# Two KAN halves in four column groups, clears on VectorE, and bank copies booked a turn ahead: one change to a macaron block on one Trainium2 core

## The chip, the cores and the metric

The kernel runs on one core of one Trainium2 chip. A core has TensorE (PE, with its weight loads listed as PEld), VectorE (DVE), ScalarE (ACT), GpSimd (POOL) and the DMA queues, the most used of which is that of SyncE (SP). The metric is the device time of one execution in microseconds; less is better. Before the change it is 1758.36 us, the median of three runs (1757.0 to 1758.48).

## The reference

The input x is 16 batch rows of 512 tokens of width 128, float32. Six residual steps follow one another:

```python
x = x + 0.5 * KAN(layernorm(x))            # first KAN
x = x + attention(layernorm(x))            # 16 heads of 8, 4 kv heads, causal, rope
x = x + 0.5 * KAN(layernorm(x))            # second KAN, the same weights
x = x + 0.5 * MoE(layernorm(x))            # 8 experts, 128 tokens each
x = x + recurrence(layernorm(x))           # a gated linear scan over tokens
x = x + 0.5 * MoE(layernorm(x))
```

The KAN is the part that the change rewrites. With M = 64 and 16 inner units for each m:

```python
s = x @ Win + bin_                          # (.., 64)
h = relu(s[..., None] * W1 + b1)            # (.., 64, 16)
g = einsum('btmh,mh->btm', h, W2) + b2      # (.., 64)
out = g @ Wout + bout
```

## The kernel before, in words

**Layout of a KAN.** One batch row is handled at a time. `norm` gives the normalised row, `turned` transposes it on PE (line 288) and ACT copies it out as `kan_xT` (line 292). One matmul (line 303) against `win`, which holds Win twice side by side, gives s for 64 values of m on 2 x 64 partitions. ACT copies it to `kan_s` (307). Eight relus on ACT (329) each make one 128 x 512 tile `kan_h`: partitions 0 to 63 hold inner unit t, partitions 64 to 127 inner unit t + 8. After every second relu, two matmuls of 64 columns (335) sum a pair of tiles into the two halves of the bank `ps_kg`; `w2d` holds diagonal weights. So a KAN has one matmul at 303 and eight at 335, that is four pairs. ACT copies `ps_kg` out as gT (340), four matmuls with `wout` follow (346), and DVE adds the result to x (349). A float32 matmul appears as two PE records in the profile.

**Attention.** `attn_in` projects q, k and v (384 to 404), applies rope on DVE, adds on POOL (399, 423), and `parts` splits q and k into three bfloat16 parts: an ACT cast (356), a POOL subtraction (359), an ACT cast (362), a POOL subtraction (365). They go to HBM and back into the operand tiles `QP` and `KP` through the SP queue. `maxima` computes scores (PE 550) and row maxima (DVE 555, 560); `weights` computes transposed scores (608), exponentials (ACT 611) and the causal mask (POOL 613); `outputs` multiplies by v with four 32-column groups side by side (631).

**Order of the work.** The order of PE, ACT, DVE and POOL is fixed by generators that emit instructions as they are stepped. One `turn` steps one bank of `weights` of batch row b and one bank of `maxima` of row b + 1, and then every side generator once: KANs, norms, projections. A row has 44 turns. I call the 44 turns with the exponentials of row b "step b". In a turn, `need` lets a side generator wait until its work fits into what is left in `room`, whose budget `MOST` per turn is 1.5 us on PE, 1.15 on DVE, 0.85 on ACT, 1.45 on POOL; `take` subtracts without waiting, at the moment when the copy is emitted. `bank` waits until one of two general PSUM banks is free and PE has room. Pacing holds in steps 0 to 15 only. One KAN at a time owns `ps_kg` (`kan_held`), and its relu t is not emitted before 15 t / 8 turns after its first.

**Stages.** Start: constants, first KANs of rows 0 to 2, `attn_in` of rows 0 and 1, with `finish(first, second)` at its end. Fill: the maxima of row 0. Steps 0 to 15. Tail: `experts`, with the recurrences beside them. `prepare` makes the constants that the first KAN waits for (`rbias`, `kcst`, `w2d`, the centred projections) and clears the padding rows of the ten `QP` tiles on POOL (493) and of the three `KP` tiles on DVE (495, 496).

Of the kernel before, what the change touches and what calls it, by code (L numbers as in the profile page):

```python
# [16 lines left out]
P = 128  # L17
# [4 lines left out]
HALF = 8  # L22
# [22 lines left out]
def tile_macaron(  # L45
# [51 lines left out]
    with ExitStack() as ph:  # L97
# [5 lines left out]
        hp = ph.enter_context(tc.tile_pool(name="p1_h", bufs=4))  # L103
# [14 lines left out]
        win = cst.tile([D, 2, M], F32, name="win")  # L118
        binc = cst.tile([P, 1], F32, name="binc")
        kw1 = cst.tile([P, HALF], F32, name="kw1")  # L120
        kb1 = cst.tile([P, HALF], F32, name="kb1")
        kw2 = cst.tile([P, HALF], F32, name="kw2")
        nc.scalar.dma_start(out=win, in_=win_in.unsqueeze(1).to_broadcast([D, 2, M]))
        nc.scalar.dma_start(out=kw1, in_=kw1_in.rearrange("m (a h) -> a m h", a=2))
        nc.scalar.dma_start(out=binc, in_=bin_in.unsqueeze(0).to_broadcast([2, M]))
        nc.scalar.dma_start(out=kb1, in_=kb1_in.rearrange("m (a h) -> a m h", a=2))
        nc.scalar.dma_start(out=kw2, in_=kw2_in.rearrange("m (a h) -> a m h", a=2))
        kb2 = cst.tile([M, 1], F32, name="kb2")
        nc.scalar.dma_start(out=kb2, in_=kb2_in.unsqueeze(1))
        wout = cst.tile([P, D], F32, name="wout")  # L130
        nc.scalar.dma_start(out=wout, in_=wout_in.unsqueeze(0).to_broadcast([2, M, D]))
# [3 lines left out]
        rbias = cst.tile([P, HALF], F32, name="rbias")  # L135

        w2d = cst.tile([P, HALF, M], F32, name="w2d")
        eye2 = cst.tile([P, M], F32, name="eye2")
# [16 lines left out]
        nc.sync.dma_start(out=rope, in_=rope_in)  # L155
        for b in range(1, B):
            load(b)
# [52 lines left out]

        def refill():
            now[0] += 1
            room.update(MOST)
# [8 lines left out]
        def bank(shape, dtype, name, work=0.0):  # L222


            while held[0] == 2 or (paced[0] and work > room["pe"]):
                yield
            room["pe"] -= work
            held[0] += 1
            return mm.tile(shape, dtype, name=name, tag="mm")
# [55 lines left out]
        def turned(src, name, pool):  # L285
            ps = yield from bank([P, NT, P], F32, "ps_t", 0.55)
            for c in range(NT):
                nc.tensor.transpose(ps[:, c, :], src[:, c, :], ident)
            yield
            dst = pool.tile([P, S], F32, name=name)  # L290
            take(act=0.6)
            nc.scalar.copy(dst, ps.rearrange("p c q -> p (c q)"))
            freed()
            yield
            yield from rest(1)
            yield
            return dst

        def kan(b):

            _, xT = yield from norm(x[b])
            ps = yield from bank([P, S], F32, "ps_s", 0.9)
            nc.tensor.matmul(ps, lhsT=win.rearrange("d a m -> d (a m)"), rhs=xT, start=True, stop=True)
            yield
            sk = w2p.tile([P, S], F32, name="kan_s")
            take(act=0.6)
            nc.scalar.copy(sk, ps)
            freed()
            yield
            while kan_held[0]:  # L310
                yield
            kan_held[0] = 1
# [4 lines left out]
            for t in range(HALF + 1):  # L317
                while now[0] < begin + 15 * t // 8:
                    yield
                pair = t % 2 == 0 and t > 0  # L320
                work = {"act": 0.8} if t < HALF else {}
                if pair:
# [4 lines left out]
                if t < HALF:  # L327
                    h = hp.tile([P, S], F32, name="kan_h")
                    nc.scalar.activation(h, sk, AF.Relu, bias=rbias[:, t : t + 1], scale=kw1[:, t : t + 1])  # L329
                    hs.append(h)  # L330
                if t == 1:
                    nc.gpsimd.tensor_tensor(x[b], x[b], kcst.unsqueeze(1).to_broadcast([P, NT, D]), ALU.add)
                if pair:
                    for i in range(2):
                        nc.tensor.matmul(pg[i * M : (i + 1) * M, :], lhsT=w2d[:, t - 2 + i, :], rhs=hs[t - 2 + i],  # L335
                                         start=(t == 2), stop=(t == HALF))
                yield
            gT = hp.tile([P, S], F32, name="kan_h")
            take(act=0.6)
# [4 lines left out]
            po = yield from bank([P, NT, D], F32, "ps_ko", 0.9)  # L344
# [3 lines left out]
            take(dve=0.7)  # L348
# [4 lines left out]
        def parts(r, dst, copies, **work):  # L353
# [4 lines left out]
            yield from need(pool=1.15)  # L358
            nc.gpsimd.tensor_tensor(r, r, dst[:, 0, :], ALU.subtract)
            yield  # L360
            yield from need(**work)
            copies(dst[:, 1, :], r)
# [12 lines left out]
        def attn_in(b, st):  # L375
# [7 lines left out]
            pa = yield from bank([P, S], F32, "ps_pa", 0.9)  # L383
            nc.tensor.matmul(pa, lhsT=wq.rearrange("k h d -> k (h d)"), rhs=xT, start=True, stop=True)
            yield
            take(dve=0.7)
            nc.vector.tensor_mul(ta, pa, rope[:, 0, :])
            freed()
            pb = yield from bank([P, S], F32, "ps_pb", 0.9)
            nc.tensor.matmul(pb, lhsT=wqr.rearrange("k h d -> k (h d)"), rhs=xT, start=True, stop=True)  # L390
            yield
            take(dve=0.7)
            nc.vector.tensor_mul(tb, pb, rope[:, 1, :])
            freed()
            pk = yield from bank([2 * KR, S], F32, "ps_pk", 0.9)
# [4 lines left out]
            take(dve=0.7)  # L400
            nc.vector.tensor_mul(ka, pk[0:KR, :], rope[0:KR, 0, :])
            pv = yield from bank([P, NT, KR], F32, "ps_v", 0.9)
# [3 lines left out]
            take(dve=0.7)  # L406
            nc.vector.tensor_mul(kb, pk[KR : 2 * KR, :], rope[KR : 2 * KR, 1, :])
            freed()
            qp_steps = parts(ta, qpart, nc.scalar.copy, act=0.6)
            step(qp_steps)  # L410
# [10 lines left out]
            def keys():  # L421
                yield from need(pool=1.25)
                nc.gpsimd.tensor_tensor(ka, ka, kb, ALU.add)
                yield
                yield from parts(ka, kpart, nc.scalar.copy, act=0.6)

            yield from together(qp_steps, keys())
# [24 lines left out]
        def center_win():  # L452
            psc = yield from bank([P, 2 * M], F32, "ps_kc0")
            centered(psc, win.rearrange("d a m -> d (a m)"))
            freed()

        def prepare():

            nc.vector.scalar_tensor_tensor(rbias, in0=kw1, scalar=binc, in1=kb1, op0=ALU.mult, op1=ALU.add)
            nc.gpsimd.memset(ones, 1.0)  # L460
            nc.gpsimd.memset(onec, 1.0)
            psc = yield from bank([1, D], F32, "ps_kc")
            nc.tensor.matmul(psc, lhsT=kb2, rhs=wout[0:M, :], start=True, stop=True)
            nc.vector.tensor_add(kcr, psc, bout)
            freed()
            yield
# [5 lines left out]
            nc.vector.tensor_add(eye2, ident[:, 0:M], ident[:, M:P])  # L472
            for u in range(HALF):
                nc.vector.tensor_scalar(w2d[:, u, :], eye2, kw2[:, u : u + 1], 0.5, ALU.mult, ALU.mult)
                if u == HALF // 2:
                    yield
# [11 lines left out]
            make_identity(nc, identb)  # L488
            nc.gpsimd.memset(causal[:, 0 : S - P], 0.0)
            make_causal_mask(nc, own, NEG)  # L490
            yield
            for i in range(NQP):
                nc.gpsimd.memset(QP[i][MXR - 32 : MXR, :, :], 0.0)
                if i < NKP:
                    nc.vector.memset(KP[i][MXR - 32 : MXR, :, :], 0.0)
                    nc.vector.memset(KP[i][MXR : MXR + 3, :, :], 1.0)
                yield
# [4 lines left out]
            yield  # L502
# [61 lines left out]
        def max_rows(b, half, maxs):  # L564
# [14 lines left out]
            pm = yield from bank([3 * H2, NT, P], BF16, "ps_m", 0.3)  # L579
# [3 lines left out]
            mr = w2p.tile([3 * H2, S], BF16, name="mr")  # L583
            take(dve=0.4)
# [34 lines left out]
        def outputs(b, st, r):  # L619
# [20 lines left out]
            pq = yield from bank([P, NT, NG, 32], F32, "ps_oq", 0.5)  # L640
# [4 lines left out]
            take(dve=0.55)  # L645
# [6 lines left out]
        def stage_out(b, st):  # L652
# [3 lines left out]
            po = yield from bank([P, NT, D], F32, "ps_o", 0.9)  # L656
# [3 lines left out]
            take(dve=0.7)  # L660
# [11 lines left out]
        def gated(k, b):  # L672
# [3 lines left out]
            ps = yield from bank([P, NT, E], F32, "ps_g", 0.9)  # L676
# [3 lines left out]
            take(dve=0.2)  # L680
# [468 lines left out]
```

## Time and profile before

The profiled execution took 1763.15 us, 1761.4 of it as span between first and last instruction, at a mean granted TensorE clock of 0.968.

| Stage (us of the span) | length | PE busy | DVE busy | ACT busy | POOL busy | PE clock |
|---|---|---|---|---|---|---|
| Start, 0 to 76.1 | 76.1 | 41.2 | 35.9 | 28.8 | 42.0 | 0.91 |
| Fill, 76.1 to 127.6 | 51.5 | 39.1 | 38.3 | 16.7 | 17.5 | 0.72 |
| Steps 0 to 2, 127.6 to 289 | 161.4 | 150.6 | 119.0 | 103.0 | 74.1 | 0.94 |
| Steps 3 to 8, 289 to 622 | 333.0 | 327.7 | 257.2 | 252.3 | 179.9 | 1.00 |
| Steps 9 to 12, 622 to 856 | 234.0 | 220.7 | 192.7 | 166.6 | 119.9 | 0.98 |
| Steps 13 to 15, 856 to 1011.3 | 155.3 | 138.5 | 93.6 | 100.4 | 78.9 | 0.97 and 0.89 |
| Tail, 1011.3 to the end | 750.1 | 718.2 | 369.2 | 328.9 | 484.3 | 0.98 |

The stages are cut where the timeline shows the first score matmul (76.1), the first exponentials of a row, and the last of row 15. Busy times are unions of an engine's instructions in the stretch; a busy PE is not PE at its peak, because matmuls overlap. In a timeline row the first number is the start, the second the time from the start to the end of the group, so what one group costs PE is read from its start to the start of the next group. An arrow in brackets names what ended an engine's idle time.

### The profile page before, as it was taken

How to read it: one execution, taken by the hardware profiler on the slowest of the kernel's cores; microseconds unless marked ns; L12 is line 12 of the kernel's file. 1: busy time of each engine (PE TensorE's matmuls, PEld its weight loads, DVE VectorE, ACT ScalarE, POOL GpSimd, SP SyncE). 2: the span in 40 equal slices, each digit the busy share in tenths (PEclk: the TensorE clock that was granted, in tenths of full speed). 3: DMA queues.
4: the chain of work that ended last, by engine and by line, in shares of the span. 5: the costliest groups of instructions: out<-in, count | busy, mean ns of one | idle time of the engine just before them, and what ended most of it. 6: DMA issues, size and time to landing. Idle time of an engine off the chain costs nothing. (4 is left out here: it accounts for less than half of the span.)

```text
span 1761.4 us, 35249 instructions
## 1 busy us (share of the span) xinstructions
PE 1636.1 (93%) x12879; PEld 1110.9 (63%) x12879; DVE 1106.0 (63%) x3594; ACT 996.6 (57%) x2000; POOL 996.6 (57%) x1463
## 2 busy tenths in 40 slices
PE   3688999999999999999989899999999999999996
PEld 2234444444444454444444389799988889999996
DVE  5477767777777788878877137734458444672222
ACT  2435667787777776776666654344443334444443
POOL 5524445455554555455434767577663677647773
PEclk8879989999999999999999899999998999999998
DMA  4110111011101111011022113233322233323342
GB/s 116 57 66 26 50 47 30 35 48 54 42 31 40 51 54 38 21 50 50 25 71 68 32 43 70 49 73 65 66 59 45 58 67 71 68 52 69 65 81 47
DMA packets 101753, 94.77 MB, mean 54 GB/s; under 512 B 11859, under 2 KB 90140, under 8 KB 101340
## 3 DMA queue, kind: packets, MB, share of 16 engines
q1 hardware_dynamic: 74512, 67.45, 12.4%
q0 software_dynamic: 26048, 24.93, 8.8%
q8 instruction: 101, 1.65, 0.4%
q14 instruction: 72, 0.59, 0.1%
q10 hardware_dynamic: 1020, 0.15, 0.0%
HBM read 58.93 MB, written 37.49 MB: 55 GB/s over the span
## 5 line engine op out<-in xcount | busy, mean ns | idle before, releaser
L611 ACT ACTIVATE pt<-ps_st 128x512 f32<-128x512 f32 (+1 forms) x704 | 386.9, 561 | 242.3 <-PE ps_st L608 236.9
L613 POOL TENSOR_SCALAR_AFFINE_SELECT pt<-pt 128x128 f32<-128x128 f32 (+2 forms) x704 | 246.9, 355 | 409.1 <-ACT pt L611 404.3
L555 DVE CUSTOM_DVE_ANT_0 below<-ps_sc,causal 128x512 bf16<-128x512 f32 (+1 forms) x512 | 316.3, 618 | 120.8 <-PE ps_sc L550 106.6
L867 ACT ACTIVATE mo<-ps_h 128x512 f32<-128x512 f32 x256 | 153.1, 598 | 260.9 <-PE ps_h L865 260.7
L791 POOL DMA_INDIRECT xg<-xnd,tokI x256 | 250.1, 977 | 79.4 <-issue 42.8
L865 PE MATMUL ps_h<-xin,mw 128*128 128x128 f32 x2048 | 279.2, 279 | 0.0
L880 PE MATMUL ps_y<-mw,mo 128*128 128x128 f32 x2048 | 273.7, 277 | 0.0
L550 PE MATMUL ps_sc<-kp,qp 72*128 72x512 bf16 (+3 forms) x1024 | 261.4, 308 | 10.2 <-DVE maxs L555 7.5
L608 PE MATMUL ps_st<-qp,kp 99*128 99x512 bf16 (+3 forms) x1024 | 261.0, 308 | 5.6 <-ACT pt L611 4.6
L912 POOL DMA_INDIRECT sum<-ye,tokI x124 | 201.8, 1628 | 100.9 <-issue 25.3
L865 PEld LDWEIGHTS ps_h<-xin,mw 128*128 128x128 f32 x2048 | 250.5, 192 | 6.4 <-issue 3.7
L880 PEld LDWEIGHTS ps_y<-mw,mo 128*128 128x128 f32 x2048 | 251.0, 193 | 2.2 <-issue 0.8
L608 PEld LDWEIGHTS <-kp 99*128 99x128 bf16 x1024 | 94.3, 101 | 204.5 <-issue 186.3
L329 ACT ACTIVATE kan_h<-kan_s,rbias,kw 128x512 f32<-128x512 f32 x256 | 206.5, 814 | 7.6 <-PE ps_kg L335 7.3
L560 DVE TENSOR_REDUCE maxs<-ps_sc 128x2 f32<-128x512 f32 (+1 forms) x192 | 130.5, 685 | 69.2 <-PE ps_sc L550 68.2
L631 PE MATMUL ps_av<-pt,va 128*32 128x512 f32 (+3 forms) x2048 | 166.8, 444 | 0.0
L335 PE MATMUL ps_kg<-kan_h,w2d 128*64 128x512 f32 x512 | 164.2, 639 | 2.2 <-ACT kan_h L329 2.2
L550 PEld LDWEIGHTS <-qp 72*128 72x128 bf16 x1024 | 97.6, 101 | 56.0 <-issue 33.8
L886 DVE TENSOR_TENSOR mo<-mo 128x128 bf16<-128x128 f32 x132 | 38.9, 295 | 137.7 <-ACT mo L871 137.5
L898 PE MATMUL acc<-mo 128*128 128x128 bf16 x1584 | 112.4, 219 | 6.3 <-DVE mo L886 6.2
L898 PEld LDWEIGHTS <-mo 128*128 128x128 bf16 x1584 | 98.9, 98 | 24.1 <-issue 22.9
L631 PEld LDWEIGHTS ps_av<-pt,va 128*32 128x32 f32 x2048 | 53.6, 109 | 92.7 <-issue 49.1
(195 smaller groups left out, 2333.3 us busy)
## 6 DMA issues: line engine op xcount, KB each, us to landing
qp<-qs SPq DMA_DIRECT2D x64, 288.0 KB
xnd<-kan_x SPq DMA_DIRECT2D x32, 256.0 KB
sum<-x SPq DMA_DIRECT2D x31, 256.0 KB
qs<-qpart SPq DMA_DIRECT2D x48, 128.0 KB
kp<-ks SPq DMA_DIRECT2D x48, 96.0 KB
x<-in_L_attn_x_dram SPq DMA_DIRECT2D x16, 256.0 KB
mw<-in_L_ffn_w_dram SPq DMA_DIRECT2D x16, 256.0 KB
xg<-xnd,tokI POOLq DMA_INDIRECT x256, 2.5
```

The costliest lines, as they stand in the source:

```text
L329: nc.scalar.activation(h, sk, AF.Relu, bias=rbias[:, t : t + 1], scale=kw1[:, t : t + 1])
L550: nc.tensor.matmul(v[:, u, 0:n], lhsT=qp[r][0 : 9 * HD, g, bass.ts(c, P)], rhs=kp[0 : 9 * HD, r, 0:n], start=alone, stop=(u == len(gs) - 1 ...
L555: nc.vector.tensor_tensor_reduce(below[:, 0:n], v[:, 0, 0:n], causal[:, S - n : S], 1.0, LOWEST, ALU.add, ALU.max, accum_out=maxs[:, c, h ...
L608: nc.tensor.matmul(v[:, u, 0:n], lhsT=kp[ROWS, r, bass.ts(c, P)], rhs=qp[r][ROWS, g, c * P : S], start=True, stop=True)
L611: nc.scalar.activation(o, v[:, :, 0:n], AF.Exp, scale=HD ** -0.5)
L613: nc.gpsimd.affine_select(out=dg, in_=dg, compare_op=ALU.is_ge, fill=0.0, base=0, pattern=[[0, len(gs)], [1, P]], channel_multiplier=-1)
L631: nc.tensor.matmul(po[32 * g : 32 * g + 32, c * P : S], lhsT=va[:, c, r, :], rhs=pt[:, g, OFF[c] : OFF[c] + n], start=(c == 0), stop=(c == ...
L791: nc.gpsimd.indirect_dma_start(out=xgs[i // E % 2][:, i % E, :], out_offset=None, in_=xnd[b], in_offset=bass.IndirectOffsetOnAxis(ap=tokI[ ...
L865: nc.tensor.matmul(pst[:, f, :], lhsT=mw1[e][:, bass.ts(f, P)], rhs=xins[i // E % 2][:, i % E, :], start=True, stop=True)
L880: nc.tensor.matmul(py, lhsT=hs[u][:, f, :], rhs=mw2[e][:, f, :], start=(f == 0), stop=(f == NF - 1))
L898: nc.tensor.matmul(acc[:, c, :], lhsT=sels[u][:, bass.ts(c, P)], rhs=yes[u][:, w, :], start=(e == 0 and c == 0 and w == 0), stop=(e == las ...
L912: nc.gpsimd.indirect_dma_start(out=sums[k, b], out_offset=bass.IndirectOffsetOnAxis(ap=tokI[g][:, n : n + 1], axis=0), in_=ye[:, b % 2 * ( ...
```

## The change

A KAN is cut by m into two halves of 32, and the 16 inner units of a half into four groups of four (`NI`, `NV`). A tile `kan_h` now holds four inner units of 32 values of m. There are two matmuls for s (one for each half), two copies out (`kan_s0`, `kan_s1`), still eight relus, and after four relus four matmuls of 32 columns go to the four quarters of `ps_kg`. The second s matmul waits for `kan_held`. `hp` has five buffers instead of four.

`parts` makes the second bfloat16 part on POOL straight from the difference, so one ACT cast of each split is replaced by one POOL subtraction. The `QP` and `KP` clears all go to DVE: those of the first pair ahead of everything, the next three `QP` at the end of `prepare`'s constants, the rest 16 turns later. `prepare` makes `w2d` before it waits for a bank; `first` is stepped before `prepare`, and 14 turns instead of 12 pass before the second row begins. `win` and `bin_` are loaded on the SP queue right behind x of row 0, `wout` and `b2` on SP behind `rope`, each in two halves; the small KAN weights stay on ACT's queue, in two halves each.

Copies out of a general bank are now booked by `owe` when the bank is claimed, and subtracted from the next turn's room, where `take` subtracted them from the room of the turn in which they are emitted.

```diff
-        hp = ph.enter_context(tc.tile_pool(name="p1_h", bufs=4))
+        hp = ph.enter_context(tc.tile_pool(name="p1_h", bufs=5))
...
+        for half in range(2):
+            cols = win_in[:, half * MH : (half + 1) * MH]
+            nc.sync.dma_start(out=win[:, half, :, :], in_=cols.unsqueeze(1).to_broadcast([D, NI, MH]))
+        inner(kw1, kw1_in)
...
         nc.sync.dma_start(out=rope, in_=rope_in)
+        out_weights()
...
+        def owe(**work):
+            for e, w in work.items():
+                owed[e] += w
         def refill():
             now[0] += 1
-            room.update(MOST)
+            room.update({e: m - owed[e] for e, m in MOST.items()})
+            owed.update(dict.fromkeys(MOST, 0.0))
...
-        def bank(shape, dtype, name, work=0.0):
+        def bank(shape, dtype, name, work=0.0, **out):
             while held[0] == 2 or (paced[0] and work > room["pe"]):
                 yield
             room["pe"] -= work
             held[0] += 1
+            owe(**out)
             return mm.tile(shape, dtype, name=name, tag="mm")
...
         def kan(b):
             _, xT = yield from norm(x[b])
-            ps = yield from bank([P, S], F32, "ps_s", 0.9)
-            nc.tensor.matmul(ps, lhsT=win.rearrange("d a m -> d (a m)"), rhs=xT, start=True, stop=True)
-            yield
-            sk = w2p.tile([P, S], F32, name="kan_s")
-            take(act=0.6)
-            nc.scalar.copy(sk, ps)
...
+            for half in range(2):
+                while half and kan_held[0]:
+                    yield
+                kan_held[0] |= half
+                ps = yield from bank([P, S], F32, "ps_s", 0.9, act=0.6)
+                nc.tensor.matmul(ps, lhsT=win[:, half, :, :].rearrange("d i m -> d (i m)"), rhs=xT,
+                                 start=True, stop=True)
+                yield
+                sh = (w1p if half else w2p).tile([P, S], F32, name=f"kan_s{half}")
+                nc.scalar.copy(sh, ps)
...
+                four = t in (U // 2, U)
...
+                if four:
+                    for half, v, h in hs:
+                        o = half * M + v % 2 * MH
+                        nc.tensor.matmul(pg[o : o + MH, :], lhsT=w2d[:, half, v, :], rhs=h,
+                                         start=(t < U), stop=(t == U))
...
-                if pair:
-                    for i in range(2):
-                        nc.tensor.matmul(pg[i * M : (i + 1) * M, :], lhsT=w2d[:, t - 2 + i, :], rhs=hs[t - 2 + i],
-                                         start=(t == 2), stop=(t == HALF))
...
         def parts(r, dst, copies, **work):
             yield from need(**work)
             copies(dst[:, 0, :], r)
             yield
             yield from need(pool=1.15)
+            nc.gpsimd.tensor_tensor(dst[:, 1, :], r, dst[:, 0, :], ALU.subtract)
+            yield
+            yield from need(pool=1.15)
             nc.gpsimd.tensor_tensor(r, r, dst[:, 0, :], ALU.subtract)
-            yield
-            yield from need(**work)
-            copies(dst[:, 1, :], r)
...
-            for i in range(NQP):
-                nc.gpsimd.memset(QP[i][MXR - 32 : MXR, :, :], 0.0)
-                if i < NKP:
-                    nc.vector.memset(KP[i][MXR - 32 : MXR, :, :], 0.0)
-                    nc.vector.memset(KP[i][MXR : MXR + 3, :, :], 1.0)
...
+            for i in range(1, NR):
+                cleared(QP[i])
+                yield
+            for _ in range(16):
+                yield
...
+        keys_cleared(0)
+        cleared(QP[0])
         run(center_win())
         first = stage_in(0, sts[0])
         for _ in range(8):
             step(first)
-        sides.append(prepare())
-        sides.append(first)
-        for _ in range(12):
+        sides.append(first)
+        sides.append(prepare())
+        for _ in range(14):
             turn()
```

## The prediction

> **What bounds the kernel now.** I read the stages first (busy time of each engine by stretch), then PE's timeline in a steady step, then PE's and DVE's in the start.
>
> ```profile
> core 0: us, PE busy (x) PEld busy (x) DVE busy (x) ACT busy (x) POOL busy (x), PEclk, DMA share, GB/s
> ...
> 289.00:622.00 333.00, 327.74 (x2362) 160.77 (x2361) 257.18 (x852) 252.26 (x462) 179.91 (x373) 1.00 0.13 43
> 622.00:856.00 234.00, 220.71 (x1571) 109.71 (x1570) 192.71 (x622) 166.57 (x307) 119.93 (x246) 0.98 0.12 41
> ...
> 1011.30:1761.40 750.10, 718.22 (x6650) 667.49 (x6648) 369.16 (x1234) 328.90 (x783) 484.32 (x439) 0.98 0.31 62
> ```
>
> In steps 3 to 8 PE is busy 98%, DVE 77%, ACT 76%: PE's order sets the length, 55.6 us a step. In steps 9 to 12 PE has 13 us of idle, DVE is at 82%. PE's timeline, steady step:
>
> ```profile
> 400.32 0.38 PE L550 MATMUL ps_sc<-kp,qp 72*128 72x512 bf16 x1
> 400.63 1.08 PE L335 MATMUL ps_kg<-kan_h,w2d 128*64 128x512 f32 x4
> 401.64 0.39 PE L608 MATMUL ps_st<-qp,kp 99*128 99x512 bf16 x1
> ...
> 402.18 1.06 PE L631 MATMUL ps_av<-pt,va 128*32 128x512 f32 x8
> 403.17 0.39 PE L608 MATMUL ps_st<-qp,kp 99*128 99x512 bf16 x1
> ...
> 410.54 1.13 PE L303 MATMUL ps_s<-kan_xT,win 128*128 128x512 f32 x2 [0.71 <-ACT kan_xT L292]
> ...
> 430.52 1.02 PE L303 MATMUL ps_s<-kan_xT,win 128*128 128x512 f32 x2
> 431.38 0.38 PE L608 MATMUL ps_st<-qp,kp 99*128 99x512 bf16 x1
> ...
> 438.09 2.02 PE L335 MATMUL ps_kg<-kan_h,w2d 128*64 128x512 f32 x4
> 440.04 0.39 PE L608 MATMUL ps_st<-qp,kp 99*128 99x256 bf16 x2
> ```
>
> From start to next start: a pair at L335 costs 1.01 us; one s matmul (L303) 0.86; four 32-column matmuls of 512 (L631) 0.99. One pair in each step takes 1.95 and one (at 423.68) 1.64: the second relu was late. The L550 ahead of a pair takes 0.31 instead of 0.22 (403.40 to 403.62).
>
> ```profile
> 33.61 1.76 DVE L496 MEMSET kp<- 3x2048 bf16 x1 [0.48 <-issue]
> 35.40 1.64 DVE L257 BATCH_NORM_STATS2 ln_st<-x 128x6 f32<-128x128 f32 x8
> ...
> 39.63 1.11 PE L288 MATMUL ps_t<-ident,kan_x 128*128 128x128 f32 x4 [10.17 <-DVE kan_x L278]
> ...
> 61.50 2.08 PE L346 MATMUL ps_ko<-wout,kan_h 128*128 128x128 f32 x8 [4.00 <-ACT kan_h L340]
> ```
>
> In the start, PE idles 10.2 us because the statistics of rows 1 and 2 stand behind DVE's clears, and 4.0 us because KAN 1's copy out stands on ACT behind the casts of `parts`.
>
> **The change part by part.** The turn counter in the code says what the order becomes: 63 turns of start become 68; each row keeps 44 turns, and no row waits at `finish`; the tail has 797 in both. So only the cost of a turn changes.
>
> *The KAN's matmuls.* Before: 4 x 1.01 + 0.86 = 4.90 us. After: 2 x 0.99 (the L631 form: same columns, type and number) + 2 x 0.86 = 3.70. That is -1.2, with two fewer switches of 0.09 -1.38 a KAN. The Trainium skill ("TensorE: Matmul & The Clock Gate", Measured speedup vs the span model) gives three column tiles a speedup of 2.38, that is 79% of ideal; by it four would cost 0.86 / 0.79 = 1.09, and a KAN save 1.18. The row has the very form, so I take 0.99; over 32 KANs the two differ by 6 us (44 or 38).
>
> *Steady steps.* Two KANs a step: -2.8. The late pairs (0.63 + 0.94) and the 0.71 ahead of L303 are 2.28 more. They stand where the old booking lets a relu (0.8) and copies (0.6 each) share a turn: ACT's room there falls to -0.35, -0.35 and -0.55 in each step, and never after. But PE that is quicker meets ACT sooner. Bounds: nothing or all of 2.28; I take half, 1.1. So -3.9 a step, -23 in steps 3 to 8.
>
> *Other steps.* Steps 0 to 2 hold 3.5 KANs (-4.8 at most, PE 93% busy): -4. Steps 9 to 12 hold 8 (-11), but the routing's top-k makes DVE end many waits there: 60%, -6.5. Steps 13 to 15 hold 3 (-4.1), PE 89% busy: -2. All steps: -35.5.
>
> *Start.* The ten clears of `QP` leave POOL (18.0 us, 1.84 each) for DVE, where the same bytes take 0.91 (the row of the `KP` clear): 9.1 more on DVE. The first 3.6 us of them lie before x of row 0 arrives (statistics at 5.21). The loads of `win` now stand behind x on SP: +1. Two s matmuls at the cold clock (2.04 each at 14.70) cost +2, but they go ahead of the wait for `wout` (12.42 before). SP issues about 8 loads of some 0.5 us ahead of row 1's x, which is not wanted before 24; ACT's queue has 8 issues instead of 9, done by 7.3, before its first copy at 9.7. `w2d` took 6.8 us for 8 small instructions beside POOL's clears; it should take about 1.5. KAN 0 then ends near 27 instead of 30, the statistics of rows 1 and 2 start near 24 instead of 35.4, the transpose at 39.63 comes near 29: -10.5. Next, KAN 1's copy out waits for one cast on ACT, not the chain cast, subtraction, cast: -3.5. Against that, six POOL subtractions of 1.15 instead of four stand ahead of the next norm's rstd (72.17 to 78.72 now): +2.3, and the later clears of 2 x 2.67 + 6 x 0.91 on DVE delay norms by about 2. Sum -9.5, bounds -15 and -3. The fill: 1.5 KANs, bound by DVE: -1.
>
> *ACT, POOL, DVE in the steps.* ACT gains 32 copies (0.58) and loses 32 casts (0.617): even. POOL gains 32 subtractions of 1.15, 2.3 a step at 54% load. Behind them queue the masks (L613), for which L631's weight loads wait, 27.7 us in 60 waits now, while PE still has matmuls in hand. Bounds 0 and 32 x 1.15 = 37; I take 0, since the masks have a turn's lead. The skill ("SBUF — State Buffer", SBUF: two separate sides) makes the pair of ports that DVE and GpSimd share an exclusive lock: a DVE instruction with two SBUF inputs waits a whole POOL instruction out. That speaks against this part: 32 x 1.15 = 37 us of DVE stalls. The row says less: L278, the form that would suffer, has a mean of 784 ns against a median of 694, so 48 x 0.09 = 4 us in the whole run, beside 57% POOL. A twentieth more POOL makes that 0.2. I take 0; by the rule 37 on DVE, perhaps a third on PE.
>
> *Tail.* One KAN: -1.4.
>
> Sum: -9.5 - 1 - 35.5 - 1.4 = -47.4. Against the profiled 1763.2 that gives 1715.8; that run lies 4.8 above the median of 1758.4, so 1711.
>
> **The rivals.**
> A (forecast, 0.47): as summed, 1711, itself 1700 to 1722.
> B (0.22): another engine takes the bound. With PE 4 us lighter a step, DVE's 43 and ACT's 42 stand in 51.7, and two banks each for scores and exponentials leave no slack: half of the steps' gain and -5 in the start, 18 + 6 = -24: 1734. For it: DVE ends L550's waits (7.5 us over 17). Against it: 77% load in steps 3 to 8.
> C (0.15): all of the 2.28 goes (-7 more in six steps, -6 in the others) and the start gives -15: 1692.
> D, slower (0.11): the four matmuls wait for four relus. A group comes due two turns after its last relu; if ACT is two relus behind (1.46 at the timeline's 0.73 apiece), 52 groups in the steps wait 76 us, against 35.5 + 12 saved: +28, 1786. It decides at 47 / 52 = 0.9 us a group. For it: pairs waited 0.63 and 0.94 already. Against it: six of eight didn't wait, and the ACT budget is now kept.
> E (0.05): the quarters don't run side by side, because each matmul reads another tile (L631's do too), or the start loses its gain to late loads: about 1756.
>
> **How the numbers follow.** Predicted 1711, case A. The range 1690 to 1740 takes in A, B and most of C, leaving D, E and a rest. No change means within 0.2%, 3.5 us, about what a measurement of this kernel can tell. Faster: A, B, C and half of E, 0.86; same 0.03; slower 0.11, D.
>
> **What would show it.** The four-column group at 0.99 to 1.0 from start to next start; s matmuls 64 instead of 32 (128 records); a steady step of 51 to 52.5 us; no late group over 1.5; the first score matmul at 66 instead of 76; tail still 750. Wrong if the step stays above 54 (B), if groups at the KAN's line wait over 0.9 (D), if PE's clock in steps 3 to 8 leaves 1.00 (each hundredth costs 3 us there), or if the first norms still wait for DVE's clears.

## The result, and the profile after

The changed kernel takes 1838.7 us, the median of four runs (1836.24 to 1841.5), against 1757.88 for the kernel before in the same comparison: a ratio of 1.0456 with a 95% interval of 1.0438 to 1.0474. It is 80.8 us slower, where 47 us of gain were predicted. The profiled execution took 1836.24 us, 73.1 more than that of before. By stage: start and fill together 125.9 us (127.6 before), steps 955.3 (883.8), tail 753.3 (750.0). The steps lose 71.5 us and the tail 3.3; start and fill gain 1.7.

The busy times of the changed kernel by stretch (start, steps 3 to 8, tail), in the columns of the first table of the prediction:

```profile
core 0: us, PE busy (x) PEld busy (x) DVE busy (x) ACT busy (x) POOL busy (x), PEclk, DMA share, GB/s
0.00:73.30 73.30, 43.10 (x145) 18.37 (x146) 39.17 (x97) 29.23 (x43) 26.41 (x44) 0.81 0.34 91
...
282.80:670.70 387.90, 339.64 (x2383) 166.92 (x2381) 263.71 (x849) 249.55 (x460) 193.37 (x384) 0.93 0.11 37
...
1081.20:1834.50 753.30, 720.87 (x6666) 669.77 (x6666) 370.32 (x1234) 330.38 (x786) 483.67 (x440) 0.98 0.30 61
```

Six steps that took 333.0 us take 387.9. DVE and ACT do what they did before (263.7 and 249.6 us against 257.2 and 252.3). PE is busy 88% instead of 98%, and its clock, 1.00 before, is 0.93. PE's timeline in step 6 shows the new KAN and a new kind of wait:

```profile
480.93 1.12 PE L426 MATMUL ps_pb<-kan_xT,wqr 128*128 128x512 f32 x2 [1.07 <-DVE rope_a L423]
...
487.64 1.06 PE L365 MATMUL ps_kg<-kan_h,w2d 128*32 128x512 f32 x8
488.64 0.39 PE L659 MATMUL ps_st<-qp,kp 99*128 99x256 bf16 x2
...
495.07 0.63 PE L659 MATMUL ps_st<-qp,kp 99*128 99x128 bf16 x4
495.50 0.63 PE L598 MATMUL ps_sc<-causal,identb 128*128 128x512 bf16 x1
```

The group of four at line 365 costs 1.00 us from its start to the next start: that term was right. But PE now stands 1.07 us before the rope projection `ps_pb`, and further on in the step score matmuls of as many columns take 0.63 instead of 0.39. The timeline of all engines around the next two waits:

```profile
489.40 0.69 DVE L612 TENSOR_REDUCE maxs<-ps_sc 128x2 f32<-128x512 f32 x1 [1.57 <-PE ps_sc L602]
...
490.01 0.25 DVE L696 RECIPROCAL rden<-ps_oq 128x16 f32<-128x16 f32 x1
490.30 0.29 DVE L697 TENSOR_TENSOR y<-ps_oq,rden 128x128 f32<-128x128 f32 x1
...
490.73 1.05 PE L438 MATMUL ps_v<-wv,kan_xT 128*128 128x32 f32 x8 [1.37 <-DVE y L697]
...
491.95 0.38 PE L602 MATMUL ps_sc<-kp,qp 72*128 72x256 bf16 x2
...
492.37 0.69 DVE L612 TENSOR_REDUCE maxs<-ps_sc 128x2 f32<-128x512 f32 x1 [1.78 <-PE ps_sc L602]
...
493.08 0.68 DVE L440 TENSOR_TENSOR rope_kb<-ps_pk,rope 32x512 f32<-32x512 f32 x1
...
493.81 1.47 PE L337 MATMUL ps_s<-kan_xT,win 128*128 128x512 f32 x2 [1.48 <-DVE rope_kb L440]
```

Read it from the bottom. `ps_s` wants one of the two general banks, the one that held `ps_pk`. The bank's last reader is `rope_kb`. Generators had emitted that reader in the same turn, behind the turn's own row maximum (492.37) in DVE's queue, and that maximum reads scores which PE had only just made (491.95). So PE makes the scores, DVE takes the maximum and then reads the bank, and only then does PE go on. For 1.48 us PE has nothing to do, and just before, for 1.78 us, DVE had nothing to do. The two engines work in turn instead of side by side.

I call this a same-turn claim: a general bank is claimed in the turn in which its last reader was emitted. They can be counted from the order in which the generators emit, without any time. Before, a steady step (5 to 8) has 1 among 21 claims; after, it has 5 among 23: `ps_pb` behind `ps_pa`'s reader, `ps_v` behind `ps_oq`'s, `ps_s` behind `ps_pk`'s, a `ps_t` behind `ps_s`'s, and the gate's `ps_g` behind `ps_t`'s. PE's list of waits names four of these readers (us in total, times, longest). None of them writes anything that the waiting matmul reads; the `kan_xT` that `ps_g` waits for is another row's (in step 6 it is copied at 521.36, the gate's own at 519.29):

```profile
PE ps_v L438 <- DVE y L697: 9.6, 7, 1.4
PE ps_s L337 <- DVE rope_kb L440: 7.4, 5, 1.5
...
PE ps_pb L426 <- DVE rope_a L423: 6.6, 6, 1.3
...
PE ps_g L727 <- ACT kan_xT L321: 4.2, 5, 0.8
```

In step 6 PE's waits at the five claims are 1.07, 1.37, 1.48, 0.31 and 0.84 us, together 5.1 of its 8.3 us of idle.

All runs together; steps and stages are from each profiled execution, the claims are those of a steady step, and each ratio is to the kernel before on the same chip. The runs h1 to h3 were made while the kernel before took 1847.89 us at a granted clock of about 0.94 instead of 0.97, and h1's profile shows the lower clock in the tail, so only their ratios, starts and steps are compared.

| run | time, us | ratio [95%] | same-turn claims | steady step | start + fill | all steps | tail |
|---|---|---|---|---|---|---|---|
| before (profiled) | 1763.15 | 1 | 1 | 55.6 | 127.6 | 883.8 | 750.0 |
| after | 1838.7 | 1.0456 [1.0438, 1.0474] | 5 | 64.3 to 67.3 | 125.9 | 955.3 | 753.3 |
| e1 after, late free | 1762.5 | 0.9995 [0.9980, 1.0009] | 0 | 55.7 | 122.0 | 882.5 | 756.8 |
| e2 after, old booking | 1780.6 | 1.0102 [1.0085, 1.0119] | 2 | 56.3 to 56.6 | 127.1 | 896.2 | 759.0 |
| e3 before, new KAN | 1768.6 | 1.0044 [1.0032, 1.0055] | 2 | 55.8 to 57.4 | 133.6 | 878.9 | 753.2 |
| e4 before, new booking | 1826.0 | 1.0348 [1.0319, 1.0378] | 1, 0, 2, 4 | 56.8 to 62.2 | 129.1 | 938.2 | 757.8 |
| f1 before, half the pairs | 1736.9 | 0.9864 [0.9836, 0.9892] | 1 | 53.5 | 129.2 | 859.1 | 745.6 |
| f2 e1, short maxima | 1727.4 | 0.9806 [0.9788, 0.9824] | 0 | 53.6 | 122.4 | 847.9 | 757.4 |
| f3 e1, half the relus | 1752.7 | 0.9951 [0.9937, 0.9965] | 0 | 55.7 to 57.2 | 122.5 | 884.0 | 753.9 |
| f4 e1, both | 1718.7 | 0.9752 [0.9730, 0.9775] | 0 | 53.2 to 54.0 | 123.3 | 842.7 | 753.1 |
| g1 before, late free | 1771.5 | 1.0066 [1.0049, 1.0084] | 0 | 59.0 | 125.1 | 891.0 | 752.2 |
| g2 g1 with new KAN | 1773.6 | 1.0069 [1.0052, 1.0086] | 0 | 56.1 to 57.1 | 132.2 | 882.2 | 757.0 |
| g3 g1 with new start | 1764.1 | 1.0020 [1.0010, 1.0029] | 0 | 59.0 | 117.2 | 895.2 | 750.6 |
| g4 g1 with both | 1757.6 | 0.9982 [0.9964, 1.0001] | 0 | 56.1 to 57.0 | 121.9 | 879.1 | 751.4 |
| h1 before, new start | 1839.1 | 0.9953 [0.9927, 0.9979] | 1 | 55.6 | 117.4 | 881.2 | 840.6 |
| h2 h1, copies on ACT | 1840.6 | 0.9967 [0.9929, 1.0004] | 1 | 55.9 | 114.6 | 883.1 | 829.0 |
| h3 relus at 14 t / 8 | 1867.5 | 1.0136 [1.0073, 1.0199] | 1 | 56.2 | 129.1 | 897.1 | 839.0 |
| h3 relus at 16 t / 8 | 1862.5 | 1.0120 [1.0056, 1.0185] | 0 | 57.6 to 57.9 | 132.6 | 888.7 | 820.4 |
| h5 h1 again | 1748.1 | 0.9922 [0.9906, 0.9938] | 1 | 55.6 | 115.7 | 884.3 | 748.2 |
| h6 h1, pairs later | 1763.6 | 1.0007 [0.9991, 1.0022] | 0 to 2 | 56.3 to 57.9 | 116.1 | 896.7 | 753.2 |

### The profile page after: what moved, and what is told of

Read it like the earlier page. It is cut to its first block, busy times and chain, and to the rows that moved or that the text cites. A ratio compares the mean times of both kernels' runs of the same rounds, so it can differ in the third digit from the quotient of the medians.

```text
span 1834.5 us, 35439 instructions
## 1 busy us (share of the span) xinstructions
PE 1643.3 (90%) x12943; PEld 1113.0 (61%) x12943; DVE 1121.2 (61%) x3606; ACT 993.3 (54%) x2000; POOL 1013.8 (55%) x1486
## 5 line engine op out<-in xcount | busy, mean ns | idle before, releaser
L602 PE MATMUL ps_sc<-kp,qp 72*128 72x512 bf16 (+3 forms) x1024 | 267.8, 315 | 19.6 <-DVE maxs L612 9.7
L659 PE MATMUL ps_st<-qp,kp 99*128 99x512 bf16 (+3 forms) x1024 | 266.1, 313 | 18.9 <-ACT pt L662 16.0
L682 PE MATMUL ps_av<-pt,va 128*32 128x512 f32 (+3 forms) x2048 | 175.9, 461 | 0.0
L294 POOL TENSOR_TENSOR ln_rstd<-ln_rstd,mhalf 128x4 f32<-128x4 f32 x96 | 100.6, 1048 | 8.0
```

Of the source, the lines that this page charges most:

```text
L602: nc.tensor.matmul(v[:, u, 0:n], lhsT=qp[r][0 : 9 * HD, g, bass.ts(c, P)], rhs=kp[0 : 9 * HD, r, 0:n], start=alone, stop=(u == len(gs) - 1 ...
L659: nc.tensor.matmul(v[:, u, 0:n], lhsT=kp[ROWS, r, bass.ts(c, P)], rhs=qp[r][ROWS, g, c * P : S], start=True, stop=True)
L682: nc.tensor.matmul(po[32 * g : 32 * g + 32, c * P : S], lhsT=va[:, c, r, :], rhs=pt[:, g, OFF[c] : OFF[c] + n], start=(c == 0), stop=(c == ...
```

## The experiments

**Which part makes the loss.** Theory 1: the loss is the same-turn claims, which the new booking brings about by moving side work to other turns. Theory 2: the loss is in the work itself, in the four-part KANs and the POOL subtractions. Four runs tell them apart. e1 keeps all of the change and takes away the same-turn claims, by letting a bank that was given back become free only at the next turn:

```diff
         def refill():
             now[0] += 1
+            held[0] -= late[0]
+            late[0] = 0
...
         def freed():
-            held[0] -= 1
+            late[0] += 1
```

> The changed kernel, with one edit: a general PSUM bank that is given back becomes free for the next claim at the end of the turn, not at once. The turn counts stay 68, 44 a row and 797. In the changed kernel 5 of a steady step's 23 claims take a bank whose reader on DVE or ACT was emitted in the same turn (1 of 21 before the change); with the edit none does. Theory 1 (PE stands at the head of its queue behind that reader, which stands behind the turn's own maximum or exponential): the five waits of 0.3 to 1.5 us in a step vanish and the clock returns to 1.00, a steady step falls from 64.5 to about 51.5, the whole to about 1700 (1680 to 1740). Theory 2 (the groups of four wait for relus, or DVE or POOL is the bound): the edit moves no work between engines, so the time stays at 1839 within 10.

It measured 1762.5 us, a ratio of 0.9995 instead of 1.0456: the loss is gone, with the same instructions. In its step 6 none of the five waits is left, the longest wait is 0.77 us, and the clock in its steady steps is 1.00 again. Theory 2 falls: the loss lies in the order, not in the work. But the time is that of before, not 1680 to 1740: something else eats the KAN's saving.

e2 takes the new booking out of the change, so that `take` is back at each copy:

```diff
-            owe(**out)
             return mm.tile(shape, dtype, name=name, tag="mm")
...
+            take(dve=0.7)
             nc.vector.tensor_mul(ta, pa, rope[:, 0, :])
```

> The changed kernel with the booking of copies as before: subtracted from the room of the turn in which the copy is emitted. All else as changed. Steady steps then hold 2 same-turn claims instead of 5. Theory 1, at about 2.9 us for each claim (64.5 less 55.6 and the 2.8 of matmuls saved, over four more claims): a steady step near 56, the whole near 1760. Theory 2: the booking costs nothing, 1839 within 10.

1780.6 us, 20 above what was expected. Its steady steps, with 2 same-turn claims, take the 56 us that were forecast (56.3 to 56.6), but its step 3 has 6 and takes 68.0, and its tail is 9 us longer than that of before. e3 puts the four-part KAN alone, with its split loads, into the kernel before:

> The kernel before with the four-part KAN alone (its matmuls, weights, their loads and constants; the bfloat16 splits, the clears, the order of the start and the booking stay as before; one small tile moves to a single buffer to make room). Steady steps hold 2 same-turn claims instead of 1. Theory 1: 2.8 us of matmuls saved a step and one more wait of about 2.9, so about the same, 1745 to 1765. Theory 2, if the groups of four or their late relus are the loss: slower by most of the 80 us, above 1800. If neither wait matters: 1720.

1768.6 us, 4 above the range of Theory 1 and far below 1800: the steps gain 4.9, the start and fill lose 6.0, the tail 3.2. e4 puts the booking alone into the kernel before, with no operation changed:

```diff
-            room.update(MOST)
+            room.update({e: m - owed[e] for e, m in MOST.items()})
+            owed.update(dict.fromkeys(MOST, 0.0))
```

> The kernel before with the new booking of copies alone (booked into the next turn when the bank is claimed). The KAN, the splits and the start stay as before. Steps 4 and 7 to 12 then hold 6 and 2, 4, 4, 4, 5, 5 same-turn claims, steps 3, 5 and 6 hold 0, 1 and 0. Theory 1: steps 8 to 12 grow by 8 to 11 us each, step 4 by 13, step 6 loses 2: 1800 to 1820, and the growth follows the claims from step to step. Theory 2: the booking is harmless by itself, 1750 to 1760, and no step stands out.

1826.0 us, above the range of Theory 1 by 6: a change that adds not one instruction costs 65 us. It also holds a comparison within one run, because the generators do not settle: steps 3 to 12 have 0, 6, 1, 0, 2, 4, 4, 4, 5 and 5 same-turn claims and take 55.4, 66.1, 59.7, 60.0, 56.8, 62.2, 64.5, 62.6, 64.8 and 63.1 us. The steps with four and more are all above 62. Step 6, with none, takes 60.0, so the claims are not all that matters. The changed kernel itself has 6 such claims in its step 3 and none in step 4, which take 68.2 and 58.8 us; but step 3 also has more side work (26 claims in all, against 20). PE's waits in step 9 are of the kind seen above:

```profile
658.81 1.17 PE L407 MATMUL ps_v<-wv,kan_xT 128*128 128x32 f32 x8 [1.07 <-DVE mr L586]
...
662.09 1.09 PE L296 MATMUL ps_t<-ident,kan_x 128*128 128x128 f32 x4 [1.46 <-DVE rope_kb L409]
...
695.36 1.10 PE L310 MATMUL ps_s<-kan_xT,win 128*128 128x512 f32 x2 [0.93 <-DVE y L647]
```

None of these matmuls reads what it waits for; it waits for its bank.

**Where the KAN's saving went.** In e1 the KAN's matmuls take 7.54 us of a steady step, against 11.49 before; the score matmuls take 24.66 against 20.54. These are sums from start to next start (lines 605 and 662, and 550 and 608), so each holds the wait of the matmul that follows. What was saved is spent there. PE's waits in e1:

```profile
PE ps_sc L605 <- DVE maxs L610: 15.3, 40, 1.2
PE ps_sc L605 <- DVE maxs L615: 10.8, 16, 3.0
PE ps_st L662 <- ACT pt L665: 8.9, 23, 0.8
```

Theory 3: with two score banks and two exponential banks, a turn is as long as its own slowest engine, and PE time is not won where DVE (3a) or ACT (3b) is longer. Theory 4: the four-part KAN gives its saving back by its own second copy or its order. f1 takes PE time out and leaves every other engine alone; two of the four pairs are left out:

```diff
-                if pair:
+                if t in (2, HALF):
                     for i in range(2):
```

> The kernel before, with two of the four pairs of KAN matmuls of each KAN left out (so half of the inner units are not summed); every relu, copy, booking and the order of all the rest stay. PE loses 4 x 1.01 = 4.0 us of each steady step (about what four-part KANs took off PE: 11.49 to 7.54 us of KAN lines a step), nothing else changes. Theory 3 (two score banks and two exponential banks: a turn is as long as its own slowest engine, so PE time taken out is mostly not won): a steady step stays at 54.5 to 55.6 us, the time 1740 to 1758. Theory 4 (PE's time is won; four-part KANs gave it back by their second copy, their POOL subtraction or their order): a steady step of 51.6 to 52.5, the time 1695 to 1715.

The steady step is 53.5, below the 54.5 of Theory 3 and above the 52.5 of Theory 4: of 4.0 us that PE lost, 2.1 became time. f2, f3 and f4 relieve DVE, ACT and both in e1. f2 takes the row maxima over half of the columns, f3 leaves out every second relu, f4 does both:

```diff
-                                below[:, 0:n], v[:, 0, 0:n], causal[:, S - n : S], 1.0, LOWEST,
+                                below[:, 0 : n // 2], v[:, 0, 0 : n // 2], causal[:, S - n : S - n // 2], 1.0, LOWEST,
```

> e1 (the change with late free) with the row maxima of the attention scores taken over the first half of the columns only (the rest is left out): 44 DVE instructions a step of 0.55 to 0.69 us become about half as long, some 11 us less DVE in a steady step, PE, ACT, POOL and the order as in e1. If DVE alone is what PE waits for (Theory 3a): step 52.1 to 53 instead of 55.7, time 1710 to 1725. If ACT (3b): 55 to 55.7, time 1750 to 1762. If both share it (3): 53.5 to 54.7, time 1730 to 1750.

> e1 with every second relu of a KAN left out (its tile is used for two matmuls): 8 x 0.83 = 6.6 us less ACT in a steady step, PE, DVE and POOL as in e1. If ACT alone is what PE waits for (3b): step 52.1 to 53, time 1710 to 1725. If DVE (3a): 55 to 55.7, time 1750 to 1762. If both share it (3): 53.5 to 55, time 1735 to 1755.

> e1 with both: maxima over half of the columns and half of the relus. Theory 3 in each of its forms: PE is left as the only long engine, the step comes to PE's busy time, 52 to 52.6 us, the time 1695 to 1720. If it stays above 54.5, neither DVE nor ACT holds PE up, and the 55.7 comes from something else (POOL's masks, the DMAs that bring the maxima back, or an order of PE's own).

Four steady steps of e1 and of f2 side by side with their busy times, first e1, then f2:

```profile
400.80:623.50 222.70, 208.33 (x1593) 104.61 (x1592) 169.21 (x569) 166.62 (x309) 129.05 (x257) 1.00 0.13 43
```

```profile
389.40:603.80 214.40, 204.91 (x1593) 104.66 (x1592) 130.68 (x570) 165.66 (x309) 130.42 (x257) 1.00 0.14 45
```

With 9.6 us less DVE a step, the step is 2.1 us shorter, though DVE was busy only 76% of e1's, and PE's waits for the row maxima fall from 33.1 to 6.4 us in the whole run. Half of the relus less on ACT change nothing in most steady steps (55.7). Both together give 53.2 to 54.0, no more than f2. So in e1's order the row maxima held back 2.1 us a step, about half of what PE had saved, and the relus none. Shorter maxima were not tried in the kernel before, so that they would gain nothing there is not shown. In f4 PE still idles 2.2 to 2.6 us a step. What is left there are mostly claims again, of banks whose readers on ACT were emitted the turn before (0.56 us twice, 0.34 and 0.28 in step 6). I made no run that takes those away.

**What late free itself costs.** e1 removed the claims, but late free is also a change of order. Four runs with late free in all of them make a square: KAN old or new, start old or new.

> The kernel before with late free alone (a general bank given back in a turn can be claimed from the next turn on). Same-turn claims of a steady step: 0 instead of 1. Theory 1 (each same-turn claim costs PE about 1.8 us a step where another engine's queue is full, as in e4): a steady step of 54 to 55.5 us against 55.6, the time 1735 to 1757. Theory 2 (late free does nothing of itself, or delays the side work): 1757 to 1775.

> The kernel before with four-part KANs and late free; old booking, old splits, old first chain. To be compared with g1, from which only the KAN differs. KAN worth by PE's lines: -3.95 us a steady step; f1 won 2.1 of 4.0 with PE lighter alone. If four-part KANs are worth what f1 won: a step 1.5 to 2.1 under g1's. If they give all of it back by their own order (two claims, two copies, one more of each): the step as g1's within 0.5. The start 8 to 11 us longer than g1's in both cases (85.7 against 76.1 in e3), so the time is g1 -30 to -10 in the first case, g1 +0 to +15 in the second.

> The kernel before with late free and the other first chain (all QP and KP clears on DVE in the new places, first stepped before prepare, 14 turns), old KAN, old booking, old splits. Start against g1: the first theory of the prediction, -10 to -4 us; if the later clears on DVE give it back, -2 to +2. Steps and tail as g1 within 5 us. Time g1 -12 to +2.

> The change with late free, the old booking and the old splits: four-part KANs, the split loads and the other first chain are what differs from g1. If KAN and start add up: g2 + g3 - g1. The start 70 to 74 us, since the split loads go with the other first chain (e1: 71.7) instead of 85.7 as in e3. If four-part KANs are worth nothing in the steps: g3 -3 to +6; if they win 2 us a step: g3 -30 to -15, the fastest of all, 1705 to 1735.

g1 was a surprise, and Theory 1 missed: one same-turn claim fewer, and the steady step goes from 55.6 to 59.0. Against before, the KAN's pairs take 10.82 us instead of 9.67, with a wait of 1.25 for a relu, and the transposed scores 10.76 instead of 9.08. In that order the new KAN is worth what the prediction said in a steady step: most of g2's are 2.9 us below g1's, and most of g4's 2.9 below g3's. Over all steps it is worth 8.8 us (g2) and 16.1 (g4), not 35.5, and it costs 9.2 us in the start (first score matmul at 74.9 in g4, 65.7 in g3), of which the fill gives 4.5 back. So the times miss what was forecast with a gain in the steps: g2 is 2 us above g1, and g4 only 6.5 below g3. The new start is worth 8.1 us in start (g3 against g1), of the 10 that the prediction saw in the first norms.

The 71.5 us that the steps lost can be laid out along these runs, each number a difference of two rows of the table: late free on before +7.2 (g1), the new KAN -8.8 (g2), the new start -3.1 (g4), new booking and splits +3.4 (e1), and taking late free away again +72.8 (after). This is one path among several: by another the booking, put in last, costs +59.1 (e2 to after). The last item brings the same-turn claims back: 5 of them, and 9.1 us of a steady step of 64.8, on average 1.8 each. It also changes the order, which alone cost 3.4 us a step in g1; no run changes the claims and nothing else, so their exact share stays open.

**Order alone.** Theory 5: apart from the claims, the turn that a piece of side work falls into sets the length of a step. h3 changes one number in the kernel before:

```diff
-                while now[0] < begin + 15 * t // 8:
+                while now[0] < begin + 14 * t // 8:
```

> The kernel before with one number changed: relu t of a KAN comes not before 14 t / 8 turns after its first, instead of 15 t / 8. The same instructions, and one same-turn claim in each steady step as before. Theory 1 alone (length follows same-turn claims and nothing else of the order): steady steps 55.6 within 0.4, time within 6 of before. Theory 5 (which turn the side work falls into sets the length as much: what DVE, ACT and PE have in the same turn): a steady step that differs by 1 to 4 us, either way, time -20 to +40.

> As h3 with 14, but 16 t / 8: a relu in every second turn, the same instructions, and no same-turn claim in steps 4 to 9 instead of one. Theory 1 alone: steady steps 53.8 to 55.6. Theory 5: a steady step that differs by 1 to 4 us either way; above 56 would show a longer step with fewer claims, as g1 did.

At 14 the step is 56.2 with the same single claim, 0.6 longer, which is less than Theory 5 asked for and more than Theory 1 allowed. At 16 it is 57.6 with no claim at all, 2.0 longer. With g1 that makes two orders without claims that are slower than before's order with one. The instructions are the same in all; so order alone costs up to 3.4 us a step, and the order of before is the best of those tried: every change that moved side work and kept PE's work made the steady step longer.

**The start, and a version that beats both.** h1 keeps the order of the steps and takes the first chain alone (its edit also moves the clears and `w2d` inside `prepare`, as in the change):

```diff
+        keys_cleared(0)
+        cleared(QP[0])
         run(center_win())
...
-        sides.append(prepare())
         sides.append(first)
-        for _ in range(12):
+        sides.append(prepare())
+        for _ in range(14):
```

> The kernel before with the other first chain alone (clears on DVE in their new places, first stepped before prepare, 14 turns of side work); old KAN and loads, old booking, old splits, no late free. If start and steps add up: the start 66 to 68.5 us (65.7 in g3) instead of 76.1, the fill as before, steady steps 55.6 with one same-turn claim, the time 1748 to 1755 against 1761 for before: faster than both kernels. If the steps lose their order because the start is shifted by two turns: steady steps 56 to 59, 1757 to 1775.

> h1 with two copies out of general banks moved from DVE to ACT (the transposed maxima, twice a row, 0.41 us each, and v, 0.28); the order and the booking as in h1. DVE 1.1 us less in a steady step, ACT as much more. By f2 (11 us less DVE: the step 2.1 us shorter) the step gains 0.2 us at most, time h1 -4 to 0; if the copies on ACT stand behind exponentials and the next claim waits for them, h1 +3 to +15.

> The same kernel as h1 (the kernel before with the other first chain alone), run again because in h1's call both kernels ran through a tail at a lower granted clock (0.86 to 0.96 in its thirds against 0.97 to 1.00). h1 showed start and fill at 117.4 us against 127.6 and steps at 881.2 against 883.8. If that holds: the time 1745 to 1754 beside 1758 to 1762 for before, ratio 0.992 to 0.997. If the gain came from the clock of that hour: ratio 0.999 to 1.001.

> h1 with the first three pairs of KAN matmuls one relu later (at t = 3, 5, 7 in place of 2, 4, 6; the last pair stays at 8). The two late pairs of a steady step (0.63 + 0.94 us of PE, waiting for the second relu) should start on time. By that alone the step loses 0.8 to 1.6 us: 54 to 54.8, time h5 -16 to -6. But same-turn claims are now 0, 2 and 1 in turn over the steps instead of 1 each, and the order shifts (Theory 5): 56 to 58 us in some steps, time h5 0 to +25.

h1 has the steady step of before to a tenth and a start and fill of 117.4 us. Run again as h5 it takes 1748.1 us, ratio 0.9922 [0.9906, 0.9938]: 13.7 us faster than before and the fastest version here that computes everything. Its start, fill and steady steps:

```profile
0.00:64.20 64.20, 41.11 (x140) 17.71 (x141) 37.41 (x95) 28.92 (x42) 23.85 (x41) 0.95 0.36 103
64.20:115.70 51.50, 39.26 (x144) 15.63 (x141) 38.36 (x115) 16.74 (x25) 17.53 (x20) 0.73 0.21 76
277.60:610.90 333.30, 328.06 (x2365) 161.13 (x2365) 257.61 (x853) 252.29 (x462) 180.26 (x373) 1.00 0.13 43
```

The first score matmul is at 64.2 instead of 76.1, and the third row is that of before. h2, with two copies moved to ACT, has steps of 55.9, 0.3 longer than h1, and a ratio that does not differ from h1's within the intervals. h6, which gives each of three pairs more lead, loses all of the start's gain: its steps are 56.3 to 57.9. The late pairs were 1.57 us of a step, but moving them moved other side work too.

## Why the prediction was wrong, point by point

**The failing step** is the sentence "So only the cost of a turn changes", and with it "the ACT budget is now kept" as a benefit of the booking. The turn counts were right (68, 704 and 797). I counted turns and priced the work in them, and asked of the new booking only what it does to ACT's room. I did not ask what a bank claim waits for when the claim and the reader of the bank fall into the same turn. The counter that gave the turns would have shown it: 5 same-turn claims a step instead of 1. What late free takes away again, claims and order together, is 72.8 us in the steps, and none of the rivals names it. A hint stood in before's own list of waits: `ps_oq` waits for `rope_kb` (2.3 us in 2) and `ps_s` for `y` (1.4 us once), neither of which it reads.

**The KAN's matmuls**, -1.38 us each, were right within 0.2. By form, the lines are these, first after, then before (busy us and mean ns):

```profile
L365 PE MATMUL ps_kg<-kan_h,w2d 128*32 128x512 f32 x512 | 82.6, 667 | 0.6 <-ACT kan_h L371 0.5
...
L337 PE MATMUL ps_s<-kan_xT,win 128*128 128x512 f32 x128 | 82.1, 732 | 10.4 <-DVE rope_kb L440 7.4 <-DVE va L448 1.1 <-ACT kan_s L341 0.7
```

```profile
L335 PE MATMUL ps_kg<-kan_h,w2d 128*64 128x512 f32 x512 | 164.2, 639 | 2.2 <-ACT kan_h L329 2.2
...
L303 PE MATMUL ps_s<-kan_xT,win 128*128 128x512 f32 x64 | 38.6, 690 | 7.3 <-ACT kan_xT L292 5.0 <-DVE y L647 1.4 <-DVE va L417 0.5
```

Together 164.7 us instead of 202.8, 1.19 less a KAN, part of it run at the lower clock. The form in the trace (0.99) was the better guide than the 1.09 estimated from the page that the prediction cites: 1.00 was measured. Rival D's mechanism is absent: the groups at L365 wait 0.6 us in the whole run, not 0.9 each. So is that of E: the quarters do run side by side.

**"Two KANs a step: -2.8"** holds only where the order is otherwise the same: -2.9 in g2 against g1. Against before's step it gave nothing in e1 and e3, and PE time taken out by itself gave 2.1 of 4.0 (f1). Rival B, another engine takes the bound and half is lost, comes nearest for this part: f2 points to DVE, at its row maxima, although DVE was at 77%. I gave it 0.22 and forecast A.

**"Half of 2.28"** for late pairs was not found. The waits at the KAN's groups did go, yet h6 shows that giving pairs more lead makes the step 0.7 to 2.3 us longer.

**"All steps: -35.5"** was +71.5, and without the same-turn claims still -1.3 (e1): what the steady steps won or lost by order was never in the sum.

**Start, -9.5** (its terms add up to -9.7): the first chain alone gave -11.9 in start (h5), better than the sum. The transpose that stood at 39.63 comes at 26.6 in h5 and at 27.8 in the changed kernel, where 29 was predicted. The term that was mis-sized is the KAN in the start, booked at +1 and +2: with its split loads it costs 9.2 (g4 against g3). The transposes of the two `attn_in`, h5 first and then after:

```profile
34.25 0.63 PE L288 MATMUL ps_t<-ident,kan_x 128*128 128x128 f32 x4 [2.96 <-DVE kan_x L278]
...
55.86 0.66 PE L288 MATMUL ps_t<-ident,kan_x 128*128 128x128 f32 x4 [1.45 <-DVE kan_x L278]
```

```profile
41.08 1.09 PE L318 MATMUL ps_t<-ident,kan_x 128*128 128x128 f32 x4 [5.40 <-DVE kan_x L308]
...
62.46 1.09 PE L318 MATMUL ps_t<-ident,kan_x 128*128 128x128 f32 x4 [7.86 <-DVE kan_x L308]
```

In the changed kernel the norms of the two `attn_in` come 5.4 and 7.9 us after PE has run dry, 3.0 and 1.5 in h5; the first score matmul is at 73.3, not 66. Which part of the new KAN delays them was not tested.

**Tail, -1.4:** it was +3.3, and +1 to +9 in the runs with the new KAN or the new booking; but g1 and h6, with neither, have +2.2 and +3.2. PE reaches the routing (`probs` transposed) 68.0 us into the tail instead of 62.5. The cause stays open.

**ACT, POOL and DVE at 0** stands for POOL: e1 has the POOL subtractions and the new booking on top of g4, and its steady step is 55.7 against 56.1 (all steps +3.4). The 37 us that the prediction worked out from the skill's rule on the shared ports left no mark on the DVE form that would suffer: `kan_x` of 128 x 512 has a mean of 738 ns in e1 and of 795 in g4.

**The sign of being wrong** was named: a step above 54, and a clock below 1.00 in steps 3 to 8. Both came, from a cause that was not in the list.

## What to carry to other kernels

Where one program hands two buffers round among several engines with queues in order, ask of every claim what stands ahead of the last reader in its own queue; if the claim and the reader are emitted in the same round, the claimer can wait for work of that same round. A booking that only decides when work is emitted can cost more than the work: count such claims in the emitted order before and after. The count warns of large losses alone (5 against 1 here); two orders without any such claim were 2.0 and 3.4 us a step slower than one with one. And time taken out of the busiest engine need not come through in full, though the next one has slack on average: at 98% PE and 77% DVE, half of it did (f1).

## What the runs showed of the hardware

I had not expected PE's clock to fall on such short waits. In step 6 of the changed kernel no wait of PE is longer than 1.48 us and PE is busy 87% of 64.5 us, but the granted clock is 0.95, in step 7 0.90; matmul rows of 0.38 become 0.63 for about 3.5 us at a time (474.08 to 477.63). In e1, with 3.6 us of idle a step and no wait above 0.8, it stays at 1.00. PE's busy time rises from 52.1 us a step in e1 to 56.2 in the changed kernel, for the same matmuls. So of the 9 us between the two steps some 4.7 are idle and some 4.1 are slower matmuls.

That such waits bring the clock down is not shown, though. Step 10 of e4 has as large a share of idle and a longer wait (1.88 us), at a clock of 1.00. Here step 6 of the changed kernel is first, step 10 of e4 second:

```profile
474.10:538.60 64.50, 56.23 (x399) 27.62 (x398) 42.90 (x143) 41.80 (x77) 32.18 (x65) 0.95 0.11 37
```

```profile
713.80:776.40 62.60, 54.74 (x393) 26.33 (x392) 51.80 (x165) 40.96 (x76) 30.61 (x64) 1.00 0.12 38
```

What sets the clock between the two stays open.
